# Norm steps at the seam of two slots, Newton steps on GpSimd, GEGLU chunks one slot later

## Chip, cores and metric

One core of one Trainium2 chip runs the whole program. The metric is the device time of one execution in microseconds; lower is better.

## What is computed

The input `x` is 4 sequences of 512 tokens of width 128, float32. First comes one causal attention block on the normalised input, with 16 heads of 64. Then six layers run on the normalised sum, each with a local attention and a GEGLU feed-forward:

```python
for i in range(DEPTH):                       # DEPTH = 6
    x = attn_layer(shift_tokens(x), Wqkv[i], q_scale[i], k_scale[i], Wo[i]) + x
    x = ffn_layer(shift_tokens(x), ln_g[i], ln_b[i], W1[i], b1[i], W2[i], b2[i]) + x

def ffn_layer(x, g, bln, W1, b1, W2, b2):
    mu = x.mean(-1, keepdims=True)
    var = ((x - mu) ** 2).mean(-1, keepdims=True)
    xn = (x - mu) / jnp.sqrt(var + 1e-05) * g + bln
    hg = xn @ W1 + b1
    a, gate = jnp.split(hg, 2, -1)
    return a * jax.nn.gelu(gate, approximate=False) @ W2 + b2
```

`shift_tokens` moves the second half of the features by one token. `attn_layer` projects to q, k and v, normalises q and k per head, rotates them, attends in windows of 32 tokens to the own window and the one before, and projects back.

## The kernel before

The program has two parts. The first (the loop over `m`) is the causal attention; the change does not touch it. The second is the six layers, and it runs as a software pipeline written out by hand. The instructions of each engine run in the order in which `slot` issues them.

A unit is 128 tokens of one sequence in one layer: `units` has 6 x 4 x 4 = 96 of them, in order of layer, sequence and tile T. `slot(n, now, last)` works on several units at once:

- `u` (number n): scores, softmax, times v, transposes of the result;
- `prev` (n - 1): output projection `project_out_2` and `residual`;
- `nxt` (n + 1): transposes of q and k;
- `new` (n + 2): projections, rotation and norms of q and k, windows of v.

Beside them, `now` and `last` are two feed-forward objects `Ffn`, each for one sequence of one layer (512 tokens). When the four units of a sequence are through, its `Ffn` becomes `now` for four slots and then `last` for the following ones. With T = n % 4, `now` does `shift` at T=0, `mean` at T=1, `var` at T=2, `scale` at T=3 (lines 753 to 756) and `chunk(0)` at T=3; `last` does `chunk(1)` at T=0, `chunk(2)` at T=1 and `out` at T=2 (lines 786 to 789).

The three norm steps are closures made by `layernorm_steps`. `mean` is one matmul with a constant 1/128 matrix (L93), a subtraction on VectorE (L95) and a square on ScalarE (L97). `var` is four one-column matmuls (L102), an addition on VectorE (L104) and `rsqrt`: a bit shift and an integer multiply-add on VectorE (L79, L80), then three Newton steps of four operations (L82 to L85) on the engine given. `scale` is four transposes of the broadcast result (L110), a product (L114) and a scale with offset (L116) on VectorE. The same `rsqrt` is used for q and k by `inverse_norms`, with 32 columns and GpSimd as its engine.

Two families of PSUM tiles matter. `one_t()` gives one-bank tiles from a ring of two:

```python
def one_t():
    return ps.tile([P, 512], F32, tag="one", name="ps_one", bufs=2)
```

The result of `project_out_2`, the norm's matmul results and every group of four transposes (`transposed`, whose result ScalarE copies out in L541) take the next tile of this ring. `two_t(k, name)` gives two-bank tiles of three fixed buffers; scores, projections, products with v, chunks and `out` use those.

The lines named later, with the tiles that the profile shows for them:

| line | what | engine |
|---|---|---|
| L442 | projections of `new` | TensorE |
| L453, L458 | square and sum of squares for q and k | ScalarE, VectorE |
| L463, L467 | `rotate` | VectorE |
| L478, L486, L557 | `add_rotated`, `over_norm`, `carry_k` | GpSimd |
| L538, L541 | transposes (`rot` of q and k, `pr`, `on`) and their copies (`qT`, `kT`, `pT`, `aT`) | TensorE, ScalarE |
| L565, L576 | mask and scores: the start of a slot on TensorE | TensorE |
| L586, L588, L594 | maximum, difference, Exp | VectorE, VectorE, ScalarE |
| L608, L617, L618 | product with v, division | TensorE, VectorE |
| L633, L641 | output projection, residual | TensorE, VectorE |
| L666, L667, L669, L671 | chunk: two matmuls, Gelu, product | TensorE, ScalarE, VectorE |
| L680, L682 | `out`: matmuls, residual | TensorE, VectorE |

Gelu and Exp need different activation tables, so ScalarE loads a table when it goes from one to the other.

Work tiles of the feed-forward (shifted input, centred input, square, Gelu, product) come from the pool `tmp` with 7 buffers. `begin(unit(n + 4))` at the start of a slot shifts the input of a coming sequence on GpSimd, and reads the `xT` that `out` of that sequence wrote in the layer before. `v_windows` issues 16 DMAs per slot on SyncE's queue; the weights of the next layer are loaded on the same queue.

Of the kernel before, what the change touches and what calls it, by code (L numbers as in the profile page):

```python
# [31 lines left out]
def body(ctx: ExitStack, tc: tile.TileContext, a, out: bass.AP):  # L32
# [5 lines left out]
    nc = tc.nc  # L38
# [3 lines left out]
    NT = S // P  # L42
# [6 lines left out]
    def tmpt(n=S):  # L49
        return tmp.tile([P, n], F32, tag="tmp", name="tmp_t")  # L50
# [23 lines left out]
    def rsqrt(v, n, eng):  # L74

        y = small.tile([P, n], F32, tag=f"y{n}", name="y")
        t = small.tile([P, n], F32, tag=f"yt{n}", name="yt")
        ti = t.bitcast(I32)
        nc.vector.tensor_scalar(ti, v.bitcast(I32), 1, None, ALU.logical_shift_right)  # L79
        nc.vector.tensor_scalar(y.bitcast(I32), ti, -1.0, 1597463007.0, ALU.mult, ALU.add)  # L80
        for k in range(3):
            eng.tensor_tensor(t, y, y, ALU.mult)  # L82
            eng.tensor_tensor(t, t, v, ALU.mult)
            eng.tensor_scalar(t, t, -0.5, 1.5, ALU.mult, ALU.add)
            eng.tensor_tensor(y if k < 2 else v, y, t, ALU.mult)  # L85

    def layernorm_steps(state, bank, inT, outT, g=None, b=None):

        def mean():
            m = bank()
            mm(m, lhsT=avg, rhs=inT(), start=True, stop=True)  # L93
            xc = state["xc"] = tmpt()
            nc.vector.tensor_tensor(xc, inT(), m, ALU.subtract)  # L95
            sq = state["sq"] = tmpt()
            nc.scalar.activation(sq, xc, AF.Square)  # L97

        def var():
            v = bank()  # L100
            for t in range(NT):
                mm(v[:, t : t + 1], lhsT=state["sq"][:, t * P : (t + 1) * P], rhs=avg[:, 0:1], start=True, stop=True)  # L102
            rs = state["rs"] = small.tile([P, NT], F32, tag="rs", name="rs")
            nc.vector.tensor_scalar(rs, v[:, 0:NT], EPS, None, ALU.add)  # L104
            rsqrt(rs, NT, nc.vector)

        def scale():
            bc = bank()
            for t in range(NT):
                nc.tensor.transpose(  # L110
                    bc[:, t * P : (t + 1) * P], state["rs"][:, t : t + 1].to_broadcast([P, P]), ident
                )
            h = state["h"] = outT()
            nc.vector.tensor_tensor(h, state["xc"], bc, ALU.mult)  # L114
            if g is not None:
                nc.vector.tensor_scalar(h, h, g, b, ALU.mult, ALU.add)  # L116

        return mean, var, scale

    xT = [None] * B  # L120
# [11 lines left out]
    with tc.tile_pool(name="s1", bufs=1) as s1, tc.tile_pool(  # L132
# [71 lines left out]
        class Rows:  # L204


            def __init__(self, b, c, t):
                self.b, self.c, self.t = b, c, t

            def scores(self):  # L210
                b, c, t = self.b, self.c, self.t
                sc = self.sc = ps1.tile([P, 2, S], F32, tag="sc", name="ps_sc", bufs=2)
                for k0 in range(0, S, S // 2):
                    for h in range(2):
                        rows = slice(h * HD, (h + 1) * HD)
                        mm(  # L216
                            sc[:, h, k0 : k0 + S // 2],
                            lhsT=qs[b, c][rows, t * P : (t + 1) * P],
                            rhs=ks[b, c][rows, k0 : k0 + S // 2],
                            start=(k0 == 0),  # L220
                            stop=False,
                            skip_group_check=True,
                        )
# [95 lines left out]
        last = len(rows) // 2  # L319
        for m in range(last + 1):  # L320
            b, c, odd = m // (2 * NC), m // 2 % NC, m % 2
            now = rows[2 * m : 2 * m + 2]
            old = rows[2 * m - 2 : 2 * m] if m else []
            if m >= 4:
                g = m // 2 - 2
# [125 lines left out]
    def square(u, j):  # L451
        u.sq = s2.tile([P, INNER], F32, tag="t1", name="sq", bufs=3)
        nc.scalar.activation(u.sq, u.p[j], AF.Square)  # L453
# [80 lines left out]
    def transposed(src, g, dst, col0):  # L534

        tp = one_t()
        for c in range(4):
            nc.tensor.transpose(  # L538
                tp[:, c * P : (c + 1) * P], src[:, (4 * g + c) * P : (4 * g + c + 1) * P], ident
            )  # L540
        nc.scalar.copy(dst[:, 4 * g : 4 * g + 4, col0 : col0 + P], tp.rearrange("p (c t) -> p c t", c=4))  # L541
# [83 lines left out]
    def transpose_o(u):  # L625
        u.aT = s2.tile([P, NC, P], F32, tag="aT", name="aT", bufs=2)
        for g in range(2):
            transposed(u.on.rearrange("p c a d -> p (c a d)"), g, u.aT, 0)

    def project_out_2(u):  # L630
        y = u.y = one_t()
        for c in range(NC):
            mm(y[:, 0:P], lhsT=wo_w[0][:, c, :], rhs=u.aT[:, c, :], start=(c == 0), stop=(c == NC - 1))  # L633
# [12 lines left out]
    class Ffn:  # L646
        def __init__(self, i, b):
            self.i, self.b, self.us, self.st = i, b, [], {}
            self.mean, self.var, self.scale = layernorm_steps(
                self.st,  # L650
                one_t,
                lambda: self.xs,
                lambda: s2.tile([P, S], F32, tag="hT", name="hT", bufs=2),
                vecs[:, i, 0:1],
                vecs[:, i, 1:2],
            )

        def shift(self):
# [43 lines left out]
    units = [Unit(i, b, T) for i in range(L) for b in range(B) for T in range(NT)]  # L702
# [6 lines left out]
    def unit(n):  # L709
        return units[n] if 0 <= n < len(units) else None  # L710

    def follower(u):
        return units[u.n + 1] if u.T + 1 < NT else None

    def begin(u):

        if u is None or u.T:
            return
        xs = s2.tile([P, S], F32, tag="xs", name="xs", bufs=2)
        shift_into(xs, xT[u.b])  # L720
        lt = layer_tables(u.i) if u.b == 0 else units[u.n - 1].lt
        for v in units[u.n : u.n + NT]:
            v.xs, v.lt, v.p = xs, lt, [None] * 3

    def do_project(u, j):
        u.p[j] = project(u, j)
        if u.b + 1 == B and u.T + 1 == NT and u.i + 1 < L:
            wpart[j] = load_part(u.i + 1, j)

    def slot(n, now, last):  # L730

        u, prev, nxt, new = unit(n), unit(n - 1), unit(n + 1), unit(n + 2)
        T = n % NT
        part[0] = n % 3
        begin(unit(n + 4))
        if u:
            scores(u)
        if new:  # L740
            do_project(new, 0)
            square(new, 0)
        if u:
            exponents(u)
        if prev:
            project_out_2(prev)
            if prev.b + 1 == B and prev.T + 1 == NT and prev.i + 1 < L:
                wo_w[0] = load_wo(prev.i + 1)
        if new:
            sum_squares(new, 0)  # L750
        if prev:
            residual(prev)
        if now and T > 0:
            (now.mean, now.var, now.scale)[T - 1]()
        if now and T == 0:
            now.shift()
        if new:
            rotate(new, 0)
            do_project(new, 2)
            v_windows(new, follower(new))  # L760
        if u:
            transpose_p(u)
        if new:
            add_rotated(new, 0)
            do_project(new, 1)
            square(new, 1)
        if u:
            times_v(u, 0)
        if new:
            sum_squares(new, 1)  # L770
        if nxt:
            transpose_q(nxt)
        if u:
            times_v(u, 1)
        if new:
            inverse_norms(new)
            over_norm(new, 0)
        if nxt:
            transpose_k(nxt)
        if new:  # L780
            rotate(new, 1)
            add_rotated(new, 1)
            over_norm(new, 1)
        if nxt:
            carry_k(nxt, follower(nxt))
        if now and T == 3:
            now.chunk(0)
        if last:
            (lambda: last.chunk(1), lambda: last.chunk(2), last.out)[T]()
        if u:  # L790
            transpose_o(u)

    with tc.manual_schedule():
        begin(units[0])
        ffns = {}
        late = norm_x1(one_t, B - 1)
        for n in range(-2, len(units) + NT + 3):
            if -2 <= n < 1:
                late[n + 2]()
            q = n // NT - 1  # L800
            if n % NT == 0 and 0 <= q < L * B:
                ffns[q] = Ffn(units[n - 1].i, units[n - 1].b)
            slot(n, ffns.get(q), ffns.pop(q - 1, None) if n % NT == 2 else ffns.get(q - 1))

def _constants(n):

# [90 lines left out]
```

## Time and profile before

| | |
|---|---|
| runs shown (3) | 2313.41, 2316.82, 2319.04 us; median 2316.82 |
| profiled execution | 2314.14 us, span 2312.4 us |
| granted TensorE clock | 0.993 |
| first part | up to about 600 us |
| the 96 slots of the layers | 620.7 to about 2280 us |
| busy time over the span | TensorE 2201.3, VectorE 1710.5, GpSimd 1436.1, ScalarE 1301.7 us |

The span is what the trace covers; the profiled execution's own time is 1.7 us longer. PE is TensorE's matmuls, PEld its weight loads, DVE is VectorE, ACT ScalarE, POOL GpSimd, SP SyncE. A line of the timeline gives start and length in us, engine, line, operation, tiles and count; in brackets stand the engine's idle time before it and what ended that. A line of the table by stretch gives the stretch, its length, the busy time and number of instructions of PE, PEld, DVE, ACT and POOL, the granted clock, the share of the DMA engines and GB/s.

### The profile page before, as it was taken

How to read it: one execution, taken by the hardware profiler on the slowest of the kernel's cores; microseconds unless marked ns; L12 is line 12 of the kernel's file. 1: busy time of each engine (PE TensorE's matmuls, PEld its weight loads, DVE VectorE, ACT ScalarE, POOL GpSimd, SP SyncE). 2: the span in 40 equal slices, each digit the busy share in tenths (PEclk: the TensorE clock that was granted, in tenths of full speed). 3: DMA queues.
4: the chain of work that ended last, by engine and by line, in shares of the span. 5: the costliest groups of instructions: out<-in, count | busy, mean ns of one | idle time of the engine just before them, and what ended most of it. 6: DMA issues, size and time to landing. Idle time of an engine off the chain costs nothing.

```text
span 2312.4 us, 81596 instructions
## 1 busy us (share of the span) xinstructions
PE 2201.3 (95%) x35088; PEld 1447.7 (63%) x35088; DVE 1710.5 (74%) x2692; ACT 1301.7 (56%) x2166; POOL 1436.1 (62%) x1897
## 2 busy tenths in 40 slices
PE   6999999999799999999999999999999999999997
PEld 3555555555366666666666666666666666666664
DVE  3665656656678788878877888877888788878773
ACT  2554544445255666666666666666566666566662
POOL 1443444444577777766767766767776767766760
PEclk9999999999999999999999999999999999999998
DMA  3000000000222233222322223223332223322220
GB/s 113 1 1 1 1 1 1 1 1 1 46 69 68 63 90 75 62 69 65 90 71 65 71 66 90 68 63 73 73 89 62 71 62 86 80 62 72 66 56 15
DMA packets 91025, 125.81 MB, mean 54 GB/s; under 512 B 25262, under 2 KB 39468, under 8 KB 90668
## 3 DMA queue, kind: packets, MB, share of 16 engines
q1 hardware_dynamic: 90236, 119.02, 21.0%
q8 instruction: 279, 4.57, 0.9%
q10 hardware_dynamic: 432, 1.57, 0.2%
q14 instruction: 78, 0.64, 0.1%
HBM read 20.41 MB, written 1.05 MB: 9 GB/s over the span
## 4 chain that ended last, share of the span: by engine, by line
PE 81%; DVE 14%; ACT 2%; issue 2%; POOL 1%; DMA 1%; SPq 0%; POOLq 0%; ACTq 0%
PE ps_proj L442 19%; PE ps_one L538 13%; PE ps_one L633 7%; PE ps_att L608 6%; PE ps_att L576 6%; PE ps_sc L216 5%; PE ps_o L287 5%; PE ps_pt L270 3%; PE ps_proj L666 3%; PE ps_proj L667 3%; PE ps_proj L680 2%; DVE yt L79 2%; PE ps_sc L229 2%; DVE t L467 2%; DVE rot L463 2%
## 5 line engine op out<-in xcount | busy, mean ns | idle before, releaser
L478 POOL TENSOR_TENSOR rot<-rot,t 128x1024 f32<-128x1024 f32 x192 | 453.9, 2364 | 193.9 <-DVE t L467 188.6
L442 PE MATMUL ps_proj<-wqkv,xs 128*128 128x512 f32 x1152 | 557.5, 607 | 15.3 <-DVE t L467 5.4
L259 POOL TENSOR_TENSOR pr<-pr,den 128x1024 f32<-128x1024 f32 x128 | 240.9, 1893 | 335.3 <-DVE den L256 333.1
L453 ACT ACTIVATE sq<-ps_proj 128x1024 f32<-128x1024 f32 x192 | 196.9, 1025 | 365.9 <-PE ps_proj L442 329.3
L486 POOL TENSOR_TENSOR rot<-rot,ss 128x1024 f32<-128x1024 f32 x192 | 365.4, 1903 | 15.0
L442 PEld LDWEIGHTS ps_proj<-wqkv,xs 128*128 128x128 f32 x1152 | 200.0, 192 | 179.6 <-issue 156.6
L458 DVE TENSOR_REDUCE ss<-sq 128x16 f32<-128x1024 f32 x192 | 233.1, 1214 | 51.4 <-ACT sq L453 50.7
L241 DVE TENSOR_REDUCE nm<-ps_sc 128x2 f32<-128x1024 f32 x128 | 156.0, 1218 | 118.7 <-PE ps_sc L229 118.7
L463 DVE TENSOR_TENSOR rot<-ps_proj,lt 128x1024 f32<-128x1024 f32 x192 | 233.4, 1216 | 0.0
L467 DVE TENSOR_TENSOR t<-ps_proj,lt 128x1024 f32<-128x1024 f32 x192 | 232.8, 1213 | 0.0
L274 ACT COPY pT<-ps_pt 128x512 f32<-128x512 f32 x128 | 75.2, 588 | 264.6 <-PE ps_pt L270 262.9
L633 PEld LDWEIGHTS ps_one<-aT,wo 128*128 128x128 f32 x1536 | 186.3, 192 | 45.3 <-issue 44.5
L538 PE MATMUL ps_one<-ident,rot 128*128 128x128 f32 x1536 | 210.2, 280 | 2.9 <-issue 1.5
L586 DVE TENSOR_REDUCE mx<-ps_att 128x16 f32<-128x1024 f32 x96 | 117.5, 1224 | 97.1 <-PE ps_att L576 95.3
L633 PE MATMUL ps_one<-aT,wo 128*128 128x128 f32 x1536 | 187.3, 275 | 0.4 <-ACT aT L541 0.4
L247 ACT ACTIVATE pr<-ps_sc,nm 128x512 f32<-128x512 f32 x256 | 175.0, 694 | 16.3 <-DVE nm L241 16.3
L82 POOL TENSOR_TENSOR yt<-y 128x32 f32<-128x32 f32 x288 | 68.9, 239 | 181.8 <-DVE y L80 166.6
L538 PEld LDWEIGHTS ps_one<-ident,rot 128*128 128x128 f32 x1536 | 164.4, 141 | 22.1 <-issue 4.6
L608 PEld LDWEIGHTS ps_att<-vw,pT 64*32 64x32 f32 x9216 | 104.0, 106 | 95.5 <-ACT pT L541 54.0
L270 PEld LDWEIGHTS ps_pt<-ident,pr 128*128 128x128 f32 x1024 | 120.0, 142 | 55.9 <-issue 45.8
L608 PE MATMUL ps_att<-vw,pT 64*32 64x65 f32 x9216 | 129.6, 226 | 26.4 <-DVE t L467 15.9
L520 ACT COPY vt<-ps_proj 128x512 f32<-128x512 f32 x192 | 103.1, 589 | 83.2 <-PE ps_proj L442 82.1
(127 smaller groups left out, 4014.8 us busy)
## 6 DMA issues: line engine op xcount, KB each, us to landing
vw<-vt SPq DMA_DIRECT2D x1152, 65.0 KB
vw_first<-vt SPq DMA_DIRECT2D x336, 65.0 KB
wqkv<-in_wqkv_dram SPq DMA_DIRECT2D x18, 512.0 KB
wo<-in_wo_dram SPq DMA_DIRECT2D x6, 512.0 KB
w<-in_w_dram SPq DMA_DIRECT2D x6, 341.0 KB
xr<-in_x_dram SPq DMA_DIRECT2D x4, 256.0 KB
out_dram<-tmp_t SPq DMA_DIRECT2D x4, 256.0 KB
w<-in_w_dram SPq DMA_DIRECT2D x12, 64.0 KB
```

Source lines behind the costliest of these rows:

```text
L259: nc.gpsimd.tensor_tensor(self.pr, self.pr, self.den.unsqueeze(2).to_broadcast([P, 2, S]), ALU.mult)
L270: nc.tensor.transpose(pt[:, k * P : (k + 1) * P], self.pr[:, h, k * P : (k + 1) * P], ident)
L442: mm(p[:, c, :], lhsT=u.xs[:, u.T * P : (u.T + 1) * P], rhs=wpart[j][:, c * 512 : (c + 1) * 512], start=True, stop=True,)
L453: nc.scalar.activation(u.sq, u.p[j], AF.Square)
L458: nc.vector.tensor_reduce(u.ss[:, j * HEADS : (j + 1) * HEADS], heads(u.sq), AX.X, ALU.add)
L463: nc.vector.tensor_tensor(heads(t0), heads(pf), lt[:, u.T, 2 * j].unsqueeze(1).to_broadcast([P, HEADS, HD]), ALU.mult)
L467: nc.vector.tensor_tensor(t1.rearrange("p (h t d) -> p h t d", t=2, d=half), pf.rearrange("p (h t d) -> p h t d", t=2, d=half)[:, :, ::-1, :],
L478: nc.gpsimd.tensor_tensor(u.r[j], u.r[j], u.t1, ALU.add)
L486: nc.gpsimd.tensor_tensor(heads(u.r[j]), heads(u.r[j]), u.ss[:, j * HEADS : (j + 1) * HEADS].unsqueeze(2).to_broadcast([P, HEADS, HD]), AL ...
L538: nc.tensor.transpose(tp[:, c * P : (c + 1) * P], src[:, (4 * g + c) * P : (4 * g + c + 1) * P], ident)
L608: mm(o[j * W : (j + 1) * W, h, c * (HD + 1) : (c + 1) * (HD + 1)], lhsT=u.pT[h * HD : (h + 1) * HD, 4 * g + c, j * W : (j + 1) * W], rhs=u ...
L633: mm(y[:, 0:P], lhsT=wo_w[0][:, c, :], rhs=u.aT[:, c, :], start=(c == 0), stop=(c == NC - 1))
```

## The change

Four things change, all in the second part.

1. `mean`, `var` and `scale` of `now` are issued as the last thing of their slot, after `transpose_o(u)`, and no longer after `residual(prev)` in the middle. They keep their slots T = 1, 2, 3.
2. The Newton steps of these norms run on GpSimd. The two integer operations before them stay on VectorE. The norms outside the layers keep VectorE.
3. The chunks move one slot later: `chunk(0)`, `chunk(1)`, `chunk(2)` at T = 0, 1, 2 of `last`, and `out` at T=3.
4. An `Ffn` lives one slot longer, and the loop over slots has one more at its end.

```diff
-    def layernorm_steps(state, bank, inT, outT, g=None, b=None):
+    def layernorm_steps(state, bank, inT, outT, g=None, b=None, eng=nc.vector):
...
-            rsqrt(rs, NT, nc.vector)
+            rsqrt(rs, NT, eng)
...
                 vecs[:, i, 0:1],
                 vecs[:, i, 1:2],
+                nc.gpsimd,
             )
...
         if prev:
             residual(prev)
-        if now and T > 0:
-            (now.mean, now.var, now.scale)[T - 1]()
         if now and T == 0:
             now.shift()
...
-        if now and T == 3:
-            now.chunk(0)
-        if last:
-            (lambda: last.chunk(1), lambda: last.chunk(2), last.out)[T]()
+        if last and T < 3:
+            last.chunk(T)
+        if last and T == 3:
+            last.out()
         if u:
             transpose_o(u)
+        if now and T > 0:
+            (now.mean, now.var, now.scale)[T - 1]()
...
-        for n in range(-2, len(units) + NT + 3):
+        for n in range(-2, len(units) + 2 * NT):
...
-            slot(n, ffns.get(q), ffns.pop(q - 1, None) if n % NT == 2 else ffns.get(q - 1))
+            slot(n, ffns.get(q), ffns.pop(q - 1, None) if n % NT == 3 else ffns.get(q - 1))
```

From the line `nc.gpsimd` on, the line numbers of the changed kernel differ from those of the kernel before by one, and by some more at the end of `slot`; the table above gives the numbers before.

## The prediction

> **What bounds the kernel now.** I read the page first (span, busy shares, chain), then the busy time by stretch for one period of four slots, then the timeline at three places of that period: the middle of the variance slot, the softmax of two slots, and the seam between two slots. A slot runs from one start of line 565 (scores of `u`) to the next; T is `n % 4`.
>
> ```profile
> span 2312.4 us, 81596 instructions
> ...
> PE 2201.3 (95%) x35088; PEld 1447.7 (63%) x35088; DVE 1710.5 (74%) x2692; ACT 1301.7 (56%) x2166; POOL 1436.1 (62%) x1897
> ...
> PE 81%; DVE 14%; ACT 2%; issue 2%; POOL 1%; DMA 1%; SPq 0%; POOLq 0%; ACTq 0%
> ```
>
> TensorE carries the chain. In the layers it runs almost without a gap, so an edit pays only where PE waits, and costs wherever it makes PE wait. The stretches below are the slots T = 0, 1, 2, 3 of one period: length, then busy time (and instructions) of PE, weight loads, DVE, ACT, POOL.
>
> ```profile
> 1305.37:1321.90 16.53, 16.49 (x329) 11.30 (x328) 12.45 (x18) 11.52 (x17) 14.32 (x24) 1.00 0.31 74
> 1321.90:1338.86 16.96, 16.96 (x331) 11.35 (x330) 12.95 (x19) 12.07 (x18) 11.64 (x18) 1.00 0.26 62
> 1338.86:1357.55 18.69, 17.83 (x340) 12.34 (x339) 16.70 (x33) 10.04 (x16) 11.86 (x18) 1.00 0.28 64
> 1357.55:1374.06 16.51, 16.46 (x333) 11.50 (x332) 14.35 (x20) 9.75 (x15) 11.36 (x16) 1.00 0.24 58
> ```
>
> Only T=2 has a hole in PE: 18.69 - 17.83 = 0.86 us. Over all periods the median slots, from one L565 to the next, are 16.54, 17.02, 18.68 and 16.56 us, together 68.80; places within a slot below are such medians too. The timeline shows where the hole is:
>
> ```profile
> 1345.32 1.90 POOL L486 TENSOR_TENSOR rot<-rot,ss 128x1024 f32<-128x1024 f32 x1
> 1345.42 1.82 DVE L79 TENSOR_SCALAR yt<-rs 128x4 int32<-128x4 int32 x1
> ...
> 1351.01 1.21 DVE L467 TENSOR_TENSOR t<-ps_proj,lt 128x1024 f32<-128x1024 f32 x1
> ...
> 1352.28 0.70 PEld L608 LDWEIGHTS ps_att<-vw,pT 64*32 64x32 f32 x64 [1.10 <-DVE t L467]
> ```
>
> The norm's shift (L79) waits out GpSimd's L486, twelve Newton steps follow, so `rotate` ends late and `times_v(u, 1)` waits for its bank. Between the medians of T=1 and T=2 the step from the q transposes to that L608 grows from 1.02 to 1.83 us: **0.81 us** of PE time in each of about 23 variance slots.
>
> The second place is the softmax. First T=0, then T=1:
>
> ```profile
> 1310.40 1.28 ACT L594 ACT_TABLE_LOAD   x1
> ...
> 1312.81 0.86 PEld L538 LDWEIGHTS ps_one<-ident,pr 128*128 128x128 f32 x8 [0.87 <-ACT pr L594]
> ...
> 1327.38 1.02 PE L93 MATMUL ps_one<-tmp_t,avg 128*128 128x512 f32 x2
> ...
> 1329.53 0.14 PEld L538 LDWEIGHTS ps_one<-ident,pr 128*128 128x128 f32 x1 [0.24 <-ACT pr L594]
> ```
>
> After a slot with a Gelu, Exp pays a table load, and in T=0 PE reaches the transposes of `pr` before Exp ends. In T=1 the mean matmul stands in between and fills that time. From L633 to the third L442 the median T=0 takes 4.64 us, T=3 (no load) 4.82 less its 0.44 of `scale`, 4.38: the unfilled load costs PE **0.26 us**.
>
> The third place is the seam between two slots, here T=0 to T=1:
>
> ```profile
> 1320.94 1.04 PE L538 MATMUL ps_one<-ident,on 128*128 128x128 f32 x8
> ...
> 1321.37 0.69 ACT L669 ACTIVATE tmp_t<-ps_proj,vecs 128x512 f32<-128x512 f32 x1
> 1321.90 0.41 PE L565 MATMUL ps_att<-band,ident 64*32 64x512 bf16 x8
> ...
> 1321.95 1.07 ACT L541 COPY aT<-ps_one 128x512 f32<-128x512 f32 x2
> ```
>
> ACT has a table load and a Gelu before the two copies of `aT`, so these run when PE is already in the next scores. Today nobody waits for them. Call E the time at which PE is free for L565: the first copy ends at the median E + 0.63 us in slots with a Gelu and at E + 0.26 in slots with `out`.
>
> **What the Trainium skill says.** "SBUF — State Buffer", section "Who interferes with whom": a `tensor_scalar` of VectorE in a two-port mode and a GpSimd instruction block each other for the whole instruction, whoever comes first. The trace agrees: L79 on `rs` takes 1.82 us beside L486, and 0.17 us in the tail with GpSimd idle. "ScalarE: Activation LUTs", section "What ACT_TABLE_LOAD costs": about 1283 ns a load; the trace has 1283 ns. "Perfetto Trace Analysis", section "Matmuls": independent groups should rotate through PSUM banks so that the evacuation of one overlaps the next. Here the `one` ring has two banks, and the waits that change with this edit are about that.
>
> **The change part by part**, per period, in PE time:
>
> 1. *Norm work leaves the middle of the slot.* The DVE hole of T=2 goes: -0.81. What is late next for L608 is nothing: with no norm (T=0) L467 ends at 8.73 us of the slot and L608 starts at 12.08. In T=1 and T=3 DVE loses 0.69 and 0.68 + 1.50 us mid-slot, worth nothing, as no PE wait stood there.
> 2. *The filler goes, and Gelu moves a slot on.* Gelu was in T = 3, 0, 1, so loads before Exp were in 0, 1, 2, and only T=0 was unfilled. Now Gelu is in 0, 1, 2, loads before Exp in 1, 2, 3, and none is filled: three times 0.26 for one, +0.52. The number of loads is unchanged.
> 3. *Where the norm now stands it needs a bank.* The order of `one_t()` tiles becomes o g0, o g1, norm; with two banks the norm's tile takes the one of o g0, and in the changed program L93 waits on ACT. PE can load its weights only when the first `aT` copy has ended: E + 0.63 + about 0.05 of signal (Exp's end to L538 in T=0), and a matmul group that starts from a stop takes about 0.07 to 0.10 longer (L102: 1.05 us after a wait, 0.95 without). So mean at T=1 +0.75, var at T=2 +0.78, scale at T=3 (after `out`) 0.26 + 0.05 + 0.06 = +0.37: together +1.90. The next slot's scores queue behind the waiting matmul on PE and all later PE work with them; no later wait gives it back, since Exp's chain starts from that slot's own matmuls.
> 4. *Chunks and `out` one slot later.* The same four or six matmul passes, elsewhere: T=2 gives 0.86 us (2.58 - 1.72) to T=3. Zero in sum. The w1/w2 loads on SP still have one slot between issue and first use, and `begin` still finds `xT` on GpSimd: L682 ended at 0.92 us of the next slot, the shift starts at 8.74 in T=0.
> 5. *Newton steps on GpSimd.* Twelve operations of 0.22 to 0.25 us with 0.08 between them (rows L82 to L85, 128x32; not seen for 128x4, so 2.5 to 3.9 us, I take 3.9). They queue after `carry_k`, from about 7.1 to 11.0 us of T=3, where `add_rotated(new, 0)` now starts at 10.84; nothing before the next slot's q transposes reads it. `scale` asks for `rs` only at about 17.6. Zero. If that cover were gone it would hit the DVE-GpSimd queue and not PE for several us.
> 6. *L104, L79, L80 and L116 at the seam.* DVE idles 0.9 us before L586 there, and L588 may end 0.9 us later before project waits for its bank (4.54 against 5.50). Against a small Newton operation of GpSimd L79 and L80 cost 0.2 to 0.4 us each, hidden. Against L486 then L478 (1.90 and 2.36) they would end 2.8 us late: 1.9 us of PE less 0.26 of Exp's wait, +1.65. L79 would start at E + 1.97 and L486 starts at E + 1.97 to 2.16: open. I take 0 and keep 1.65.
>
> Sum: -0.81 + 0.52 + 1.90 = **+1.61 us** a period, slots of about 16.28, 18.03, 18.05 and 18.05. There are 22 full periods: +35.4. The first has no Gelu and gains 0.81 against three stalls of 0.37: +0.3. The tail takes over one chunk (1.72) which the slot 7 loses: 0. Total +36 on the profiled execution's 2314.14 is 2350; the median of the runs shown is 2.7 above that execution, so **2352**.
>
> **The rivals.**
>
> *L79 loses the port at the seam* (part 6): +1.65 in each of 23 slots on top, +38, 2390; half of the slots, 2371. For it speak the 0.0 to 0.2 us between the two starts; against it, that DVE, arriving within the last small operation, would be next.
>
> *The bank is free in time, and the change is faster.* One mechanism: if the `aT` copy ended before PE reached the norm (before E, where it now ends at E + 0.63), part 3 is 0 and -0.81 + 0.52 = -0.29 a period remains, -7 us: 2310. It decides from a total stall below 0.29 us a period. For it: with `out` the copy is only 0.26 late. Against it: 0.62 to 0.63 in nearly every Gelu slot.
>
> *Nothing measurable*: stall and gain cancel at 0.29 to 0.5 us a period, 2317 to 2321.
>
> **How the numbers follow.** My case (stall, port won) 0.62, with 2337 to 2365; port lost in many slots 0.22, 2365 to 2390; smaller stall but slower 0.04; same 0.03; faster 0.09. The range leaves out the faster case and the far end of the port case: 2330 to 2380. About 0.2% (4.6 us) is what a measurement of this kernel can tell from no change.
>
> **What would show it.** Right: L93 and L102 at the end of T=1 and T=2 show a wait for ACT `aT` L541, about 0.7 us, L110 about 0.3; L608 has no wait for DVE L467; L538 on `pr` waits for Exp in T = 1, 2, 3 and not in 0; slots near 16.3, 18.0, 18.0, 18.0. Wrong: slots T=1 to 3 of 17.3 and no wait at L93, or T=3 near 19.7 with L442 waiting for L588, which is the port case.

## Result and the profile after

The changed kernel takes **2377.5 us** (median of 6 runs, 2373.3 to 2382.7) against 2317.2 before (6 runs, 2313.4 to 2319.0). The ratio is **1.026, 95% interval 1.0244 to 1.0275**: slower by 60 us. The prediction was 2352, with a range of 2330 to 2380. The profiled execution took 2375.81 us.

From the page of the changed kernel, span, busy time and the shares of the chain:

```profile
span 2374.0 us, 81496 instructions
...
PE 2211.1 (93%) x35056; PEld 1442.4 (61%) x35088; DVE 1680.8 (71%) x2404; ACT 1303.9 (55%) x2166; POOL 1497.2 (63%) x2185
...
PE 75%; DVE 10%; ACT 9%; issue 3%; POOL 2%; DMA 1%; SPq 0%; POOLq 0%; ACTq 0%
```

PE has the same work and is busy for a smaller share. Part of the chain has moved from PE (81% before, now 75%) to ACT (2% before, now 9%): PE now waits for ScalarE. From the first L565 to the last the layers take 1706.12 us against 1644.57, which is 61.55 of the 61.7 us between the two profiled executions; the first part and the tail take no part in it. The table by stretch shows one period, slots T = 0, 1, 2, 3, and the next T=0 (columns as in the prediction):

```profile
1332.10:1348.07 15.97, 15.97 (x330) 11.10 (x330) 13.47 (x18) 9.11 (x13) 13.13 (x18) 1.00 0.36 90
1348.07:1366.50 18.43, 17.78 (x331) 11.66 (x330) 13.37 (x19) 12.64 (x19) 13.05 (x24) 1.00 0.31 75
1366.50:1385.01 18.51, 17.45 (x338) 11.94 (x338) 13.13 (x18) 12.15 (x17) 11.64 (x18) 1.00 0.22 50
1385.01:1404.58 19.57, 17.81 (x336) 12.09 (x336) 16.49 (x20) 9.67 (x14) 13.70 (x28) 1.00 0.25 60
1404.58:1422.44 17.86, 16.20 (x329) 11.17 (x328) 13.64 (x18) 9.01 (x13) 15.55 (x19) 1.00 0.24 59
```

The hole that before stood in T=2 alone is now in T = 1, 2 and 3 (18.43 - 17.78 = 0.65 us, 1.06, 1.76), and in every second T=0 (0 in the first line, 1.66 in the last). Over all slots the medians are 16.79, 18.23, 17.96 and 19.54 us, the means 16.96, 18.17, 17.75 and 19.01; the means before were 16.62, 17.13, 18.67 and 16.81. So T=0 lost 0.33 us on average, T=1 lost 1.04, T=2 won 0.92 and T=3 lost 2.20. A part of the last two is the end of the program alone: the last layer's `out` and `finish` stood in slots 90 and 94 before (22.57 and 18.55 us long, now 17.86 and 15.34), and one of them now stands in slot 91 (17.36 before, 21.56 now).

The view of who waited for whom gives engine, waiting tile and line, what it waited for, then total us, number of times and the longest:

```profile
PEld ps_one L538 <- ACT pr L594: 51.4, 56, 1.9
...
PEld ps_one L93 <- ACT aT L541: 19.1, 23, 0.8
...
PEld ps_one L102 <- ACT aT L541: 19.0, 23, 0.9
...
PE ps_proj L442 <- DVE pr L588: 16.3, 11, 1.6
```

The second and third rows are the bank wait of part 3 of the prediction, for each of the 24 sequences but the last, which comes after the last slot with transposes of `on`. The last is the wait that was named as the sign of the lost port. The timeline at the seam from T=1 to T=2 shows the bank wait:

```profile
1363.80 1.04 PE L538 MATMUL ps_one<-ident,on 128*128 128x128 f32 x8
...
1364.23 0.69 ACT L670 ACTIVATE tmp_t<-ps_proj,vecs 128x512 f32<-128x512 f32 x1
1364.82 1.06 ACT L541 COPY aT<-ps_one 128x512 f32<-128x512 f32 x2
1365.45 1.12 PE L93 MATMUL ps_one<-tmp_t,avg 128*128 128x512 f32 x2 [0.61 <-ACT aT L541]
1366.50 0.41 PE L565 MATMUL ps_att<-band,ident 64*32 64x512 bf16 x8
```

Gelu (L670) holds back the two copies of `aT`; the mean matmul needs the bank of the first one, and the next slot's scores (L565) stand behind it. The start of T=3 in the same trace shows the port:

```profile
1385.12 0.16 DVE L104 TENSOR_SCALAR rs<-ps_one 128x4 f32<-128x4 f32 x1 [0.83 <-PE ps_one L102]
...
1385.31 1.90 POOL L486 TENSOR_TENSOR rot<-rot,ss 128x1024 f32<-128x1024 f32 x1
1385.31 1.92 DVE L79 TENSOR_SCALAR yt<-rs 128x4 int32<-128x4 int32 x1
...
1387.16 2.35 POOL L478 TENSOR_TENSOR rot<-rot,t 128x1024 f32<-128x1024 f32 x1
1387.27 2.27 DVE L80 TENSOR_SCALAR y<-yt 128x4 int32<-128x4 int32 x1
...
1390.70 1.22 DVE L588 TENSOR_TENSOR pr<-ps_att,mx 128x1024 f32<-128x1024 f32 x1
...
1392.07 1.96 PE L442 MATMUL ps_proj<-wqkv,xs 128*128 128x512 f32 x4 [1.43 <-DVE pr L588]
```

Two operations on 512 numbers last as long as the GpSimd operations beside them, 1.92 and 2.27 us. The softmax work behind them (L586, L588) is late, and PE's projection waits 1.43 us. L79 was held up like this, and PE waited, in 11 of the 21 slots T=3 from slot 11 on, most of them 19.5 to 19.6 us long. In the other ten L79 came through in 0.17 us, L80 alone was held up (about 1.8 us), and PE had no such wait; six of these took 18.0 to 18.4 us, and the other four were longer for other reasons (a gap as in the next view in two of them, the last layer's `finish` in one).

The hole in T=0 was in no part of the prediction. The timeline of PE there:

```profile
1404.80 1.51 PE L576 MATMUL ps_att<-kT_first,qT 64*32 64x64 f32 x122
1407.97 0.31 PE L576 MATMUL ps_att<-kT_first,qT 64*32 64x64 f32 x6 [1.66 <-issue]
```

In the middle of a run of 128 equal score matmuls PE stops for 1.66 us, and no semaphore ends the stop ("issue").

### The profile page after: what moved, and what is told of

It reads as the page before. It is cut to its first block, busy times and chain, and to the rows that moved or that the text cites. A ratio compares the mean times of both kernels' runs of the same rounds, so it can differ in the third digit from the quotient of the medians.

```text
span 2374.0 us, 81496 instructions
## 1 busy us (share of the span) xinstructions
PE 2211.1 (93%) x35056; PEld 1442.4 (61%) x35088; DVE 1680.8 (71%) x2404; ACT 1303.9 (55%) x2166; POOL 1497.2 (63%) x2185
## 4 chain that ended last, share of the span: by engine, by line
PE 75%; DVE 10%; ACT 9%; issue 3%; POOL 2%; DMA 1%; SPq 0%; POOLq 0%; ACTq 0%
PE ps_proj L442 20%; PE ps_one L538 12%; PE ps_att L608 6%; PE ps_one L633 6%; PE ps_att L576 5%; PE ps_sc L216 5%; PE ps_o L287 4%; PE ps_pt L270 3%; ACT L670 2%; ACT kT L541 2%; DVE y L80 2%; PE ps_sc L229 1%; PE ps_proj L681 1%; ACT tmp_t L670 1%; PE ps_pj L186 1%
## 5 line engine op out<-in xcount | busy, mean ns | idle before, releaser
L442 PE MATMUL ps_proj<-wqkv,xs 128*128 128x512 f32 x1152 | 557.9, 608 | 28.5 <-DVE pr L588 16.3
L486 POOL TENSOR_TENSOR rot<-rot,ss 128x1024 f32<-128x1024 f32 x192 | 365.6, 1904 | 15.0
L442 PEld LDWEIGHTS ps_proj<-wqkv,xs 128*128 128x128 f32 x1152 | 198.4, 192 | 184.3 <-issue 168.1
L82 POOL TENSOR_TENSOR yt<-y 128x32 f32<-128x32 f32 (+1 forms) x360 | 83.7, 232 | 310.5 <-DVE y L80 291.7
L467 DVE TENSOR_TENSOR t<-ps_proj,lt 128x1024 f32<-128x1024 f32 x192 | 233.3, 1215 | 0.0
L538 PE MATMUL ps_one<-ident,rot 128*128 128x128 f32 x1536 | 210.4, 279 | 3.1 <-issue 2.1
L617 DVE RECIPROCAL rden<-ps_att 128x8 f32<-128x8 f32 x192 | 39.1, 204 | 232.1 <-PE ps_att L608 232.1
L538 PEld LDWEIGHTS ps_one<-ident,rot 128*128 128x128 f32 x1536 | 164.4, 141 | 22.2 <-issue 4.7
L586 DVE TENSOR_REDUCE mx<-ps_att 128x16 f32<-128x1024 f32 x96 | 117.1, 1220 | 59.6 <-PE ps_att L576 59.5
L608 PEld LDWEIGHTS ps_att<-vw,pT 64*32 64x32 f32 x9216 | 109.3, 105 | 72.9 <-ACT pT L541 52.5
L608 PE MATMUL ps_att<-vw,pT 64*32 64x65 f32 x9216 | 134.0, 225 | 6.0 <-issue 5.6
```

The source lines that it names most:

```text
L442: mm(p[:, c, :], lhsT=u.xs[:, u.T * P : (u.T + 1) * P], rhs=wpart[j][:, c * 512 : (c + 1) * 512], start=True, stop=True,)
L467: nc.vector.tensor_tensor(t1.rearrange("p (h t d) -> p h t d", t=2, d=half), pf.rearrange("p (h t d) -> p h t d", t=2, d=half)[:, :, ::-1, :],
L486: nc.gpsimd.tensor_tensor(heads(u.r[j]), heads(u.r[j]), u.ss[:, j * HEADS : (j + 1) * HEADS].unsqueeze(2).to_broadcast([P, HEADS, HD]), AL ...
L538: nc.tensor.transpose(tp[:, c * P : (c + 1) * P], src[:, (4 * g + c) * P : (4 * g + c + 1) * P], ident)
L608: mm(o[j * W : (j + 1) * W, h, c * (HD + 1) : (c + 1) * (HD + 1)], lhsT=u.pT[h * HD : (h + 1) * HD, 4 * g + c, j * W : (j + 1) * W], rhs=u ...
```

## Experiments

Ratios are to runs of the kernel before that were made beside those of the experiment.

**1. Norm steps back in the middle of the slot** (changed kernel with one block moved back).

```diff
         if prev:
             residual(prev)
+        if now and T > 0:
+            (now.mean, now.var, now.scale)[T - 1]()
...
-        if now and T > 0:
-            (now.mean, now.var, now.scale)[T - 1]()
```

> Changed kernel with the three norm steps put back to the middle of the slot; chunks and out stay one slot later, Newton steps stay on GpSimd. Theory (the seam costs: no filler before Exp's load, bank wait, port at the seam): every load before Exp (T=1,2,3) is again filled by mean, var, scale, T=0 has no load (-0.26), the DVE hole of T=2 is gone (-0.81): slots 16.28, 17.02, 17.01, 17.42, -1.07 us a period, about 2292. Rival 'GpSimd queue': Newton on GpSimd delays add_rotated and with it PE, then most of the +60 stays, above 2340. Rival 'chunks': moving Gelu and out a slot costs by itself (fetch of PE instructions, ACT), then above 2330.

Measured: 2284.43 us (4 runs), ratio **0.9868 (0.9853 to 0.9882)**. One period from its table by stretch:

```profile
1365.10:1381.19 16.09, 16.09 (x331) 11.17 (x330) 11.23 (x15) 9.76 (x15) 14.69 (x17) 1.00 0.33 74
1381.19:1398.10 16.91, 16.91 (x332) 11.50 (x331) 14.34 (x20) 12.06 (x18) 12.72 (x22) 1.00 0.47 128
1398.10:1414.97 16.87, 16.87 (x338) 11.88 (x337) 14.25 (x21) 11.52 (x17) 13.87 (x29) 1.00 0.35 90
1414.97:1432.61 17.64, 17.45 (x335) 11.93 (x334) 15.18 (x21) 10.02 (x16) 12.03 (x20) 1.00 0.28 68
```

PE's busy time is the length of the slot in the first three lines: the holes of these slots are closed, and T=3 keeps 0.19 us. The place of the norm steps is worth 93 us (2377.5 - 2284.4), and with them in the middle the rest of the change is a gain of 31. This version beats both kernels, and both rivals (above 2340 and above 2330) are refuted. The medians of its slots are 16.07, 16.99, 16.97 and 17.42 us: those expected, but for T=0, which is 0.21 shorter.

**2 and 3. The two other edits alone** on the kernel before: chunks and `out` one slot later (as in the diff of the change), and the Newton steps on GpSimd:

```diff
                 vecs[:, i, 1:2],
+                nc.gpsimd,
             )
```

> Kernel before with only the chunks and out one slot later (norm mid-slot, Newton on VectorE). Theory: only the unfilled load of T=0 goes, -0.26 x 23 = -6, about 2311; the hole of T=2 (0.81) stays. Rival 'chunks': above 2330. Rival 'GpSimd queue': 2317, nothing.

> Kernel before with only the Newton steps of the layer norms on GpSimd (norm mid-slot, chunks where they were). Theory: L608 in T=2 no longer waits for rotate, -0.81 x 23 = -19, about 2298. Rival 'GpSimd queue': add_rotated waits behind twelve operations and L80 behind L486, PE waits at the q transposes or at the bank of square, above 2317 and up to 2360.

Measured: 2301.38 us, ratio 0.994 (0.9928 to 0.9953), and 2301.34 us, ratio 0.9937 (0.9923 to 0.995). Newton on GpSimd did what was expected of it in T=2: the step from the q transposes to L608 went from 1.83 to 1.02 us (14.5 us in all, 19 expected). The later chunks gave 14 us where 6 were expected: T=0 lost its wait for Exp (0.27 us a slot, the 6 us); about 0.1 to 0.15 us a slot more went in L608, for which no cause was found. The two gains, 14.4 and 14.5, make 28.9 of the 31.4 us of experiment 1. So two of the change's edits are gains, and only the move of the norm steps is a loss.

**4. The port** (changed kernel; L79, L80 and the Newton steps of T=2's `var` are issued in the middle of T=3).

```diff
             nc.vector.tensor_scalar(rs, v[:, 0:NT], EPS, None, ALU.add)
-            rsqrt(rs, NT, eng)
+            if not split:
+                root()
...
+        if now and T == 3:
+            now.st["root"]()
         if now and T == 0:
             now.shift()
```

> Changed kernel, but rsqrt (L79, L80 and the Newton steps) of the layer norm is issued after residual in T=3 instead of at the seam of T=2 and 3; the norm's matmuls, L95, L97, L104 and scale stay at the seam. Theory: L79 and L80 no longer stand before L586, so L442 of T=3 waits no more for L588: T=3 slots all near 18.0 instead of 18.1 or 19.6, mean gain 0.9 us x 23 = -21, about 2356; the bank waits at L93, L102, L110 stay. Rival 'the excess of T=3 and T=0 is fetch of PE instructions': no change, 2370 or more.

Measured: 2361.34 us, ratio 1.0199 (1.0185 to 1.0213), 16.2 us less than the changed kernel; the rival (2370 or more) is refuted. T=3 fell from 19.54 to 18.24 us (median). Its timeline at the start of T=3 (lines behind L106 are 6 higher here):

```profile
1450.29 0.16 DVE L104 TENSOR_SCALAR rs<-ps_one 128x4 f32<-128x4 f32 x1 [0.75 <-PE ps_one L102]
...
1451.95 1.22 DVE L592 TENSOR_REDUCE mx<-ps_att 128x16 f32<-128x1024 f32 x1 [1.50 <-PE ps_att L582]
...
1456.31 0.48 DVE L79 TENSOR_SCALAR yt<-rs 128x4 int32<-128x4 int32 x1
```

DVE is free when the scores end, and L79 now takes 0.48 us. The port's price in the changed kernel is 16 us. The bank waits and the gaps of T=0 stayed. The 5 us by which the expectation of 2356 was missed are in T=0, whose mean rose from 16.96 to 17.17 us: in four of its slots (24, 52, 60, 80) the granted clock fell to 0.5 for 3.4 us soon after the gap, and they took 19.5 to 19.8 us; in the changed kernel this happened in one (80). The table by stretch shows it for slot 52:

```profile
1543.80:1547.20 3.40, 3.40 (x9) 1.84 (x8) 2.02 (x2) 0.65 (x1) 3.22 (x5) 0.51 0.02 5
```

**5. Newton steps at the seam on VectorE** (changed kernel without the argument `nc.gpsimd`).

> Changed kernel with the Newton steps of the layer norm on VectorE again (norm at the seam, chunks later). Theory: twelve more operations of 0.20 us stand before L586 in T=3, so L588 ends at least 2.4 us later than in the changed kernel and L442 waits that long: +2.4 x 23 = +55, about 2432, or more where they wait for GpSimd too. Rival 'the move to GpSimd is what costs': faster than the changed kernel, below 2370.

Measured: 2516.65 us, ratio 1.0885 (1.0867 to 1.0902), 85 us above the 2432 of the theory, which had left "more" open. The rival is refuted. T=3 takes 25.77 us (median). Its timeline:

```profile
1521.26 2.27 DVE L80 TENSOR_SCALAR y<-yt 128x4 int32<-128x4 int32 x1
...
1523.58 1.91 POOL L486 TENSOR_TENSOR rot<-rot,ss 128x1024 f32<-128x1024 f32 x1
1523.76 1.75 DVE L83 TENSOR_TENSOR yt<-yt,rs 128x4 f32<-128x4 f32 x1
...
1530.03 3.75 PE L442 MATMUL ps_proj<-wqkv,xs 128*128 128x512 f32 x4 [5.50 <-DVE pr L588]
```

A product of two small SBUF tiles (L83) also waits out a GpSimd operation, 1.75 us. The Trainium skill, "SBUF — State Buffer", section "Who interferes with whom", says so for VectorE operations with two SBUF inputs, and the row agrees. PE waits 5.50 us, and after it the four matmuls take 3.75 us instead of 1.96. The table by stretch gives the reason, the granted clock of 0.50 in these 3.75 us:

```profile
1530.03:1533.78 3.75, 3.75 (x5) 1.58 (x6) 3.44 (x4) 0.94 (x1) 0.17 (x1) 0.50 0.02 4
```

Every slot T=3 from slot 7 on has such a stretch, in most of them 6.8 us long, and all four runs have a mean clock of 0.964 to 0.966 against 0.99 or so in the others. So the miss has two parts, a wait at L442 of about 5.5 us where some 2.4 more than in the changed kernel were expected, and a slower PE after it. With Newton on VectorE the move to the seam costs another 139 us.

**6 and 7. Square in place of Gelu**, in the changed kernel and in the one before. The result of the feed-forward is another; in these traces no wait for Exp behind a table load is left.

```diff
-            nc.scalar.activation(g[0:fn, :], gp[0:fn, 0, :], AF.Gelu, bias=vecs[0:fn, i, 6 + f : 7 + f])
+            nc.scalar.activation(g[0:fn, :], gp[0:fn, 0, :], AF.Square, bias=vecs[0:fn, i, 6 + f : 7 + f])
```

> Changed kernel with Square in place of Gelu (same instruction form, no table load for it nor for Exp; the feed-forward's result is another). Theory: Exp's wait goes in T=1,2,3 (3 x 0.26), the aT copy ends at about E + 0.26 instead of E + 0.63 (2 x 0.37), and var comes early enough for L79 and L80 to meet only small GpSimd operations (about 0.9 in T=3): -2.4 us a period, about 2320. Rival 'the bank wait has nothing to do with the Gelu before the copy': only Exp's 0.78 goes, about 2359.

> Kernel before with Square in place of Gelu. Theory: only T=0's unfilled load goes, -0.26 x 23 = -6, about 2310, since mean, var (and no load at T=3) covered the others. Rival 'table loads cost everywhere': all 48 loads of a layer pass sit on the path, some -40, below 2290.

Measured: 2334.47 us, ratio 1.0094 (1.0079 to 1.0109), and 2314.42 us, ratio 0.9999 (0.999 to 1.0009); neither rival (2359, and below 2290) came. In the changed kernel the wait for Exp went, the stall at L93 shrank from 0.70 to 0.47 us, and L79 and L80 came through at once in 19 of the 21 slots T=3. The timeline of that kernel at the seam from T=2 to T=3:

```profile
1364.24 1.05 ACT L541 COPY aT<-ps_one 128x512 f32<-128x512 f32 x2
1364.86 1.05 PE L102 MATMUL ps_one<-avg,tmp_t 128*128 128x1 f32 x8 [0.37 <-ACT aT L541]
...
1366.15 0.17 DVE L79 TENSOR_SCALAR yt<-rs 128x4 int32<-128x4 int32 x1
1366.35 0.17 DVE L80 TENSOR_SCALAR y<-yt 128x4 int32<-128x4 int32 x1
1366.37 1.91 POOL L486 TENSOR_TENSOR rot<-rot,ss 128x1024 f32<-128x1024 f32 x1
```

L80 starts 0.02 us ahead of L486. So the 1.9 us of the port turn on some tenths of a microsecond in the arrival of `rs`. The 14 us by which this kernel missed its expectation are spread over all slots: by the means T=0 to T=3 gained -0.15, 0.45, 0.54 and 0.93 us, where 0, 0.63, 0.63 and 1.16 were expected. The gaps of T=0 stayed, but they stand in both kernels. In the kernel before, T=0 won 0.32 us (0.26 expected), and T=1 lost 0.49, about half of it to gaps without a semaphore at the places that experiment 8 explains (5.1 us in T=1 before, 10.3 here): nothing in sum.

**8. The gaps: 128 PE instructions at the start** (changed kernel, 64 transposes of the identity ahead of the first part).

```diff
+        for _ in range(4):
+            pad = pt_bank()
+            for k in range(16):
+                nc.tensor.transpose(pad[:, (k % 4) * P : (k % 4 + 1) * P], ident, ident)
         mean, var, scale = norm_x(0)
```

> Changed kernel with 64 transposes of the identity on PE added at the very start (128 PE instructions, half of a 16 KB piece of the instruction stream), before the first transposes of x; 0 to 20 us longer at the start. Question: the gaps of 1.2 to 2.3 us inside L576 of T=0 that no semaphore ends (slots 8, 16, 24, 32, 44, 52, 60, 80, 88 of 24 T=0 slots, 15.6 us in all against 1.8 before). Theory 'place in the instruction stream': the gaps move to other slots (12, 20, 28, 36, 40, ...) or vanish, and the layers' time from the first to the last L565 changes by up to 15 us. Rival 'timing alone': same slots, same 15 us.

Measured: 2376.56 us, ratio 1.0273 (1.025 to 1.0295), the time of the changed kernel, but with the gaps in other slots: 4, 12, 20, 28, 48, 56, 64, 76, 84 instead of 8, 16, 24, 32, 44, 52, 60, 80, 88. Its timeline of PE in slot 44, where the gap shown above was, and in slot 48:

```profile
1395.72 1.57 PE L580 MATMUL ps_att<-kT_first,qT 64*32 64x64 f32 x128
...
1467.36 1.43 PE L580 MATMUL ps_att<-kT_first,qT 64*32 64x64 f32 x115
...
1470.03 0.34 PE L580 MATMUL ps_att<-kT_first,qT 64*32 64x64 f32 x13 [1.24 <-issue]
```

Where a gap falls depends on the place in PE's stream of instructions, and not on the data or the slot.

That place can be counted. The trace has 71,483 records of PE in the changed kernel (35,056 matmuls, 35,088 weight loads, 1,339 of the sequencer), and the page's row of the DMA queue that brings PE's instructions (packets, MB, share of the engines) is

```profile
q8 instruction: 279, 4.57, 0.9%
```

71,483 / 256 = 279.2: one packet of 16 KB for 256 instructions. The Trainium skill, "Runtime: NRT & Kernel Launch", section "Instruction fetch mechanics", gives this size of a block, and says that the cost of crossing into the next is mostly hidden. Counting records through the trace, every gap of over 1 us in the score runs of the twelve kernels profiled (ten have such gaps) stands at one and the same number modulo 256 within its kernel (161 or 193; 161 where 32 matmul records are missing from the trace), which I take as the first instruction of a block. The first instruction of a block never comes earlier than 2.14 us after the start of what I take as its packet. In the changed kernel the score run of a slot T=0 (256 instructions) has a gap in all 9 slots, from slot 8 on, where the block begins at the 165th instruction or later, and in none of the 13 where it begins at the 155th or earlier; in the padded kernel in all 9 (0.65 to 2.00 us) from the 170th on, and in none of 13. Four slots are 10.5 blocks long, hence every second T=0. All gaps at block beginnings in T=0 together: about 2.5 us before, 18.0 after, 16.5 with the pad, 4.2 in experiment 1. The mostly hidden cost came out here when the packet started late: in the nine slots it starts 0.3 to 1.7 us after the slot's first L565, in the 13 others at least 4.8 us ahead of it.

**9. The bank wait** (kernel of experiment 4; in T=1 and T=2 the first four transposes of `on` go ahead of the chunk).

```diff
+        early = u and T in (1, 2)
+        if early:
+            transpose_o(u, 0)
         if last and T < 3:
             last.chunk(T)
...
-            transpose_o(u)
+            if not early:
+                transpose_o(u, 0)
+            transpose_o(u, 1)
```

> Previous kernel e4_root_mid, and in T=1 and T=2 the first group of the transposes of `on` is issued before the chunk, so that its aT copy comes before the Gelu on ACT and its bank is free when the norm asks. Theory: the waits of L93 and L102 for aT (0.75 each) go, the first group waits 0.4 for its own bank (kT copy): -0.35 x 46 = -16, about 2345. Rival 'those waits are only where PE waits for something else': they reappear at the next matmul and nothing is gained, 2361.

Measured: 2347.72 us, ratio 1.0147 (1.0129 to 1.0165), 13.6 us less than experiment 4; the rival (nothing gained) is refuted. Its timeline in T=1:

```profile
1351.46 0.66 PE L544 MATMUL ps_one<-ident,on 128*128 128x128 f32 x4 [0.24 <-ACT kT L547]
...
1354.11 1.02 PE L93 MATMUL ps_one<-tmp_t,avg 128*128 128x512 f32 x2
```

L93 waits no longer; the early transposes wait 0.24 us for the copy of `kT` instead. Two waits of 0.70 became two of about 0.3 to 0.4: the bank wait is what the order of the tiles in the ring of two makes it.

**10. Why the packets came late** (kernel of experiment 4; in T=3 `scale` goes ahead of `out`).

```diff
+        if now and T == 3:
+            now.scale()
         if last and T == 3:
             last.out()
         if u:
             transpose_o(u)
-        if now and T > 0:
-            (now.mean, now.var, now.scale)[T - 1]()
+        if now and T in (1, 2):
+            (now.mean, now.var)[T - 1]()
```

> The kernel with the roots of the norm in the middle of T=3, and in T=3 the whole of scale (four transposes L116, product, scaling) issued ahead of the feed-forward's out and of the transposes of on, instead of behind them. The instructions of a slot are the same in number, so the blocks of 256 instructions in which TensorE's stream is fetched fall on the same places of the score runs. The wait of the norm's transposes for the aT copy (0.40 us in T=3) goes, -9 us against the 2361 of that kernel; in its place they wait at most 0.24 us for the copy of kT, +0 to +5. Theory A: a matmul that waits right ahead of slot T=0 also holds back TensorE's reading of its stream, so that the packet with the next block starts late; then the gaps at block boundaries in T=0 (18.0 us in all) fall to some 3 us as in the kernel before, another -15: 2337 to 2342, T=0 near 16.2. Theory B: the late packets have another cause; the gaps of 1 to 2 us stay in slots 8, 16, 24, 32, 44, 52, 60, 80, 88: 2352 to 2357.

Measured: 2354.41 us, ratio 1.0185 (1.0166 to 1.0204). The gaps at block beginnings in T=0 fell from 18.0 to 7.0 us, though the blocks begin at nearly the same places (0 to 20 instructions later in these nine slots); from slot 8 on only slots 8, 44 and 80, where they begin at the 254th instruction or later, keep about 1 us. In the other six of the nine the packet now starts 2.4 to 3.0 us ahead of the slot. T=0 fell from 17.17 to 16.35 us on average; the dips of the clock in slots 24, 52, 60 and 80 went too. Slot 52 in the kernel before, in the changed kernel, and here (timelines of PE):

```profile
1513.94 1.06 PE L576 MATMUL ps_att<-kT_first,qT 64*32 64x64 f32 x87
1515.40 0.66 PE L576 MATMUL ps_att<-kT_first,qT 64*32 64x64 f32 x41 [0.40 <-issue]
```

```profile
1551.02 1.33 PE L576 MATMUL ps_att<-kT_first,qT 64*32 64x64 f32 x107
1553.93 0.42 PE L576 MATMUL ps_att<-kT_first,qT 64*32 64x64 f32 x21 [1.57 <-issue]
```

```profile
1531.28 1.57 PE L582 MATMUL ps_att<-kT_first,qT 64*32 64x64 f32 x128
```

So theory A held for the gaps: with no wait of PE right ahead of slot T=0 most packets start in time. Experiment 5 narrows this down. There L110 stands at the end of T=3 as in the changed kernel and waits for the same copy, and yet only slots 8 and 44 have a gap of over 1 us. What differs is an instruction of PE's sequencer. In the changed kernel L110 needs a tile of GpSimd (`rs`) beside ScalarE's copy, and an EVENT_SEMAPHORE stands ahead of it; with Newton on VectorE there is none in the layers. The rows for L110, changed kernel and experiment 5 (number, duration in ns, first and last start):

```profile
L110 PEldq EVENT_SEMAPHORE  x26: 51/51/51, 18.8 to 2357.3; - x26
...
L110 PEldq EVENT_SEMAPHORE  x2: 51/51/51, 18.8 to 619.1; - x2
```

In the changed kernel 22 slots T=3 have it, 0.66 us (median) before the next slot; in experiment 10 it comes 4 us before it. The five profiled kernels with this instruction at the end of T=3 (the changed one, experiments 4, 6, 8 and 9) have 8 to 10 gaps of over 1 us in T=0, the seven others none to two. This is read from traces; no run changes that instruction alone.

On the time theory A fell short, 7 us instead of 19 to 24, for two reasons. The norm's transposes wait for the copy of `kT` (0.33 us) as long as they did for `aT`, so T=3 stayed at 18.21. And once, in the tail, `scale` now follows the root in the same slot and waits 4.2 us for GpSimd's L85; the tail from the last L571 on takes 53.8 us instead of 47.0.

## Why the prediction was right, and where it was not

The main mechanism was right: the norm steps at the seam meet a bank that ScalarE has not emptied, and PE waits for ScalarE's copies. The case that came is another than the one taken as likeliest (bank wait, port won, 2337 to 2365): it is the one with the port lost in many slots, which had a chance of 0.22. The measured time is 25 us above the point and 2.5 below the upper end of the range, and 15 of these 25 us come from a cost that the prediction did not have; that the range still held is in part luck. Point by point:

1. **Middle of the slot, -0.81.** Confirmed: the step from the q transposes to L608 in T=2 went from 1.83 to 1.02 us, and no L608 waits for L467. Experiment 3 gets the same from the Newton steps alone.
2. **Unfilled table loads, +0.52.** Confirmed in form: L538 on `pr` waits for Exp in T=1 and T=2 and not in T=0; in T=3 it waits where L79 was not held up, and where it was, the wait at L442 covers Exp. The step from L442 to L538 is 1.92 us with the wait and 1.72 without, and the transposes take 0.06 longer after it: the 0.26 of the prediction.
3. **Bank wait, +1.90.** Confirmed: the step from the transposes of `on` to the norm's matmul is 1.65 us for L93 against about 0.95 without a wait, 1.64 for L102, 1.37 for L110: +0.70, +0.69 and +0.40, together 1.79. Experiment 9 halved the first two by the order of tiles alone.
4. **Chunks later, 0.** Not quite: alone they give 14 us (experiment 2), of which 6 are the wait for Exp in T=0, counted under point 2.
5. **Newton on GpSimd, 0.** Confirmed: twelve operations of 0.20 us with 0.08 between them, from 6.47 to 9.77 us of T=3 (medians), nobody waiting. It has a side that was not looked for: it puts a wait for GpSimd's `rs` on PE's sequencer ahead of L110 (experiment 10).
6. **L79 and L80 at the seam, taken as 0, kept at 1.65: this is the term that was mis-sized.** It is 16 us over the kernel (experiment 4), some 0.7 us a period: L79 was held up in 11 of 21 slots, and each of these took about 1.4 us longer (19.57 against 18.15). The argument that DVE would be next in the arbitration was wrong: L79 and L486 both started at 1385.31, and L79 waited. The rival "half of the slots", 2371, is what happened in this part.

What no point had: **the gaps of T=0**. The prediction gave T=0 16.28 us, 0.26 less than before; the gaps at block beginnings added 18.0 - 2.5 = 15.5 us over 24 slots, 0.65 a slot, and 0.65 - 0.26 = 0.39 is near the 0.33 found. 2352 + 16 + 15 = 2383; T=2 was by its mean 0.29 us a slot better than predicted, -7, nearly all of it in the slots 90 and 94 of the program's end; measured 2377.5.

The rival with the free bank (2310) is refuted: the wait stood in 23 of the 24 sequences. Experiment 1 is not that case, though it is faster, since there the norm steps also fill the time of the table loads again.

Open: the 8 us of experiment 2, and how a waiting instruction of the sequencer holds up the packet, which no trace shows.

## What to carry to other kernels

Before a matmul is moved behind a group of transposes, count the tiles of its ring: with two banks it waits for the copy of the group before last, and that copy stands behind whatever the copying engine does at that time. Tiny VectorE operations of 0.17 to 0.20 us took 1.75 to 2.27 here when they met a long GpSimd operation; where the two starts lie within 0.2 us of each other, the full price should be put into the sum with its share of slots, not left at nothing. A wait for a second engine on a matmul can cost more than the wait itself: look for an EVENT_SEMAPHORE ahead of it. A gap of PE that no semaphore ends should be counted against the instruction stream before it is put down to the work around it.

## What was not expected of the hardware

- TensorE's stream comes in blocks of 256 instructions, one packet each. The first instruction of a block came at the earliest 2.14 us after its packet's start, and 128 score matmuls with their 128 weight loads last about 1.6 us. When the packet starts late, PE stops, for up to 2.3 us (about 29 us of such stops over the layers of the changed kernel, 17 before, 16 in experiment 1).
- Moving one group of four transposes and its wait away from the start of a slot took most of these stops away (18.0 to 7.0 us in T=0), and putting 128 instructions ahead of the whole program moved them to the slots between. The kernels with many such stops are those in which PE's sequencer has a waiting instruction of its own just ahead of the slot.
- After a wait of 5.50 us four matmuls of 128x512 took 3.75 us instead of 1.96, at a granted clock of 0.50. After a stop of 1.84 us in slot 52 of experiment 4 the clock was 0.51 for 3.4 us; not every stop of that length was followed by such a dip.
